# Weighted sums of sampled values by matmuls with matrices of weights, and edge counting in two column halves

## The chip, the cores and the metric

The kernel runs on one core of a Trainium2 chip. TensorE (PE, with its weight loads PEld), VectorE (DVE), ScalarE (ACT), GpSimd (POOL) and SyncE (SP) each work through instructions of their own in order. Transfers are issued by SP, ACT and POOL and run on 16 shared DMA engines. The time is device microseconds of one execution, the median over runs: 6115.38 us over 17 runs before, from 6101.3 to 6127.13.

## The reference

The reference is a network of two blocks on x of 2 images, 64 by 64 places, 256 channels. Each block has a token mixer ("conv") and a feed-forward part ("ffn"), added to x. The change touches the first mixer, a deformable attention, and the first step of the first ffn, a graph attention over 1,048,576 edges.

The first mixer normalizes x, makes queries, keys and values by a matrix and a 3 by 3 depthwise convolution, and has 8 groups of 32 channels. Group g samples keys and values at 9 points around each place, base distance r = 2g + 1, moved by learned offsets, with bilinear weights and clamped coordinates:

```
out = v00 * (1 - wx) * (1 - wy) + v01 * wx * (1 - wy) + v10 * (1 - wx) * wy + v11 * wx * wy
...
k_list.append(_flow_warp(k_map[:, sl], off) * mask[:, None])
v_list.append(_flow_warp(v_map[:, sl], off) * mask[:, None])
...
attn = jnp.einsum('bgpc,bgpkc->bgpk', qh, k)
attn = jax.nn.softmax(attn, axis=-1)
out = jnp.einsum('bgpk,bgpkc->bgpc', attn, v)
...
return out @ proj_w + proj_b
```

The edges' end points are indices of nodes, of which this x has 8192 (2 x 64 x 64). An edge to a higher index is dropped, and a higher source is taken as the last node; the kernel needs, for each node, how many edges with such a source end there.

## The kernel before, in words

`metaformer` (line 2228) runs the parts in order: `attention0`, `project_out`, then the router, the experts and the second block, which the change leaves alone.

**The front** is `static_maps` (209): layernorm and the query, key and value matrix per four tiles of 128 places (228 to 259), then depthwise convolutions, on DVE for queries and values (`dwconv`, 199), on PE for keys (335 to 363), and a convolution on PE that gives offsets and masks (364 to 378). It writes maps to DRAM: `qd`, `kd` (channel, x, image, y), `vd` (rows of both images in turn, with 16 repeated rows and columns as a border) and `offd`. POOL clears the padded query tile q0 (276) and copies the borders of `vd` (`borders`, 309). Between its steps it calls `next(edges)`: `sort_edges` (1047) takes 512 edges a partition at a time, selects words on DVE, and counts nodes: for each edge a one-hot row `ol` of 128 (the node's low 7 bits) and `oh` of 64 (the high bits), in bf16 with 16 edges interleaved, are multiplied into one PSUM tile `psc` (1118). DVE makes `ol` and `oh` (1115, 1116).

**The attention** is `static_attention` (381). If no offset reaches beyond one place, a sample at distance r is a weighted sum over 3 by 3 whole places around it, so each group needs 81 fixed shifts (group 0, whose points adjoin, 25). The groups go in the order 1 to 7, then 0, through three steps, and stage n holds three lanes: values of the nth group, weights of the next, dots of the one after. The lanes' steps are merged by a fraction of the way through each lane (427 to 431), and the framework's scheduler then fixes each engine's order. Two stages come before the first values.

- `group_dots` (440): queries times keys of the same x, for all pairs of rows y and ky: matmuls of 32 rows by 64 columns, 192 moving columns, on four tiles of the array; two images by two halves; ACT copies PSUM into `stage` (480); `store` writes to the DRAM tile `dots`.
- `group_weights` (506): `pick` reads diagonals of `dots` in runs of 32 floats; tents (the bilinear weights) times dots are summed to logits; softmax; POOL multiplies weights and tents into `wt`, 9 by 9 weights a place (`along_x`, 632). Group 0 joins equal shifts (`join`, 638).
- `group_values` (682): for each of 9 row shifts `load` reads the shifted value rows (711); `run` multiplies a window of 16 columns by 3 weights on DVE (733), adds one or two of the three products on POOL (740), and adds the rest into four PSUM accumulators by matmuls with the identity (746). ACT spreads the weights into `wp` (717). `end` copies the sums and stores them in `od`, one row a place (756, 758).

If an offset does reach beyond one place, a loop (`gathered`) computes the attention another way; it doesn't run with these inputs. Its test separates the attention from what follows.

**The projection** is `project_out` (772): per four tiles it loads `od` and x, transposes on PE (790), copies on ACT (792), multiplies (795) and adds to x (796). The layernorm of the router follows it tile by tile.

## Time and profile before

| | |
|---|---|
| median of 17 runs | 6115.38 us (6101.3 to 6127.13) |
| the profiled execution | 6101.96 us, span 6100.2 us |
| busy in the span | PE 4954.1 us (81%), DVE 3728.4 (61%), POOL 2269.2 (37%), ACT 1442.5 (24%) |
| front, 0 to 1005 us | `static_maps` and `sort_edges` |
| two stages without values, 1005 to 1228 us | dots of groups 1 and 2, weights of group 1 |
| eight value stages, 1228 to 3158 us | the groups 1 to 7 and 0 |
| projection, 3158 to 3275 us | with the router's layernorm among it |
| the rest, 3275 to 6100 us | unchanged by the change |

In the lines that follow, a group of instructions is written as line, engine, operation, out<-in, sizes and count, then busy time and mean duration of one in ns, then the idle time of the engine just before them and what ended it. PE's durations contain a part that overlaps the next matmul; the pace is read from starts in order of time. An f32 matmul appears as two PE instructions.

### The profile page before, as it was taken

The page shows a single profiled execution, that of the slowest core. Times are in us where ns is not written, and L with a number is a line of the kernel's source. Part 1 is how long each engine was busy: PE and PEld are TensorE (multiplying, and loading weights), DVE is VectorE, ACT ScalarE, POOL GpSimd, SP SyncE. Part 2 cuts the span into 40 slices and gives each one's busy share as a digit, 9 for nine tenths or more (in the row PEclk, how much of TensorE's full clock was granted, in tenths as well). Part 3 has the DMA queues.
Part 4 walks back from the last instruction along what each step waited for, and adds up shares of the span by engine and source line. Part 5 has one row for each costly group of instructions (what it writes and reads, how often), then busy time and mean ns, then how long its engine had stood idle before and what let it go on. Part 6 is the DMA issues. An engine that isn't in the chain of part 4 may idle for free. (4 is left out here: it accounts for less than half of the span.)

```text
span 6100.2 us, 68586 instructions
## 1 busy us (share of the span) xinstructions
PE 4954.1 (81%) x23911; PEld 2983.2 (49%) x23911; DVE 3728.4 (61%) x6085; ACT 1442.5 (24%) x2580; POOL 2269.2 (37%) x1994
## 2 busy tenths in 40 slices
PE   9999985598998988998877686089976788869993
PEld 5645784333343433433334343078853444448882
DVE  7897866375888887899955577011136555542223
ACT  3221111223333323221003000022223444412220
POOL 0000000064786877788840773700035111110016
PEclk9989986577988978899989798599987888879996
DMA  5436667545546555564243100277742000038885
GB/s 163 147 114 155 135 53 128 122 104 118 131 125 143 126 138 134 143 136 96 59 111 59 7 6 6 104 234 225 225 136 74 21 21 22 21 131 268 262 271 180
DMA packets 946768, 740.49 MB, mean 121 GB/s; under 512 B 611795, under 2 KB 833247, under 8 KB 935265
## 3 DMA queue, kind: packets, MB, share of 16 engines
q1 hardware_dynamic: 725004, 488.35, 32.1%
q10 hardware_dynamic: 185812, 167.81, 10.2%
q0 software_dynamic: 35584, 79.71, 4.4%
q8 instruction: 197, 3.23, 0.2%
q14 instruction: 171, 1.39, 0.1%
HBM read 469.87 MB, written 276.15 MB: 122 GB/s over the span
## 5 line engine op out<-in xcount | busy, mean ns | idle before, releaser
L746 PE MATMUL acc<-prod,ident 128*128 128x512 f32 x2716 | 1389.3, 657 | 156.2 <-POOL prod L740 132.7
L733 DVE TENSOR_TENSOR prod<-vt,wp 128x1536 f32<-128x1536 f32 (+1 forms) x796 | 1334.4, 1732 | 210.3 <-PE acc L746 154.5
L740 POOL TENSOR_TENSOR prod<-prod 128x512 f32<-128x512 f32 x1010 | 1307.0, 1319 | 413.5 <-DVE prod L733 393.4
L746 PEld LDWEIGHTS acc<-prod,ident 128*128 128x128 f32 x2716 | 523.4, 204 | 822.6 <-issue 546.0
L480 ACT COPY stage<-dot 128x384 f32<-128x384 f32 (+1 forms) x640 | 482.8, 840 | 1065.9 <-PE dot L473 868.2
L473 PE MATMUL dot<-kt,qt 32*64 32x192 f32 (+1 forms) x5888 | 511.5, 415 | 154.8 <-ACT stage L480 85.8
L1501 PE MATMUL ps_h<-xgT,w1t 128*128 128x256 f32 x2240 | 540.4, 389 | 33.4 <-DVE xgT L1496 23.8
L473 PEld LDWEIGHTS dot<-kt,qt 32*64 32x64 f32 x5888 | 279.9, 164 | 545.2 <-ACT stage L480 271.1
L1509 PE MATMUL ps_y<-w2t,hT 128*128 128x256 f32 x2240 | 506.3, 379 | 0.0
L1512 DVE TENSOR_TENSOR y<-ps_y,b2t 128x256 f32<-128x256 f32 x280 | 118.8, 424 | 627.3 <-PE ps_y L1509 461.5
L1501 PEld LDWEIGHTS ps_h<-xgT,w1t 128*128 128x128 f32 x2240 | 415.9, 192 | 112.2 <-DVE xgT L1496 33.3
L1509 PEld LDWEIGHTS ps_y<-w2t,hT 128*128 128x128 f32 x2240 | 425.6, 190 | 57.9
L1504 ACT ACTIVATE hT<-ps_h,b1t 128x256 f32<-128x256 f32 x560 | 259.1, 474 | 818.9 <-PE ps_h L1501 752.7
L1234 PE MATMUL ps<-oh,ol 128*128 128x512 f32 (+1 forms) x864 | 328.5, 544 | 93.8 <-DVE oh L1227 93.8
L2127 POOL DMA_INDIRECT xs<-tn,sloti x128 | 124.8, 975 | 611.3 <-DVE slot L2125 522.1
L1596 POOL DMA_INDIRECT back<-ys,back_row x128 | 124.7, 974 | 585.3 <-DVE run L2112 539.7
L207 DVE SCALAR_TENSOR_TENSOR cv<-pad,colt,cv 128x2048 f32<-128x2048 f32 x128 | 296.5, 2339 | 0.0
L1234 PEld LDWEIGHTS ps<-oh,ol 128*128 128x128 f32 x864 | 170.4, 198 | 251.6 <-issue 211.1
L349 PE MATMUL ps_k<-padk,diag 128*128 128x512 f32 x576 | 267.2, 619 | 19.7 <-ACT km L354 19.3
L1494 PE MATMUL ps_x<-ident,xg 128*128 128x128 f32 x560 | 85.7, 276 | 218.3 <-DMA xg<-xs 218.3
L1118 PE MATMUL psc<-oh,ol 128*128 128x64 bf16 x1792 | 239.1, 305 | 22.0 <-DVE oh L1116 22.0
L1118 PEld LDWEIGHTS <-ol 128*128 128x128 bf16 x1792 | 225.2, 148 | 52.2 <-issue 40.9
(392 smaller groups left out, 5961.2 us busy)
## 6 DMA issues: line engine op xcount, KB each, us to landing
w1t<-in_W SPq DMA_DIRECT2D x140, 512.0 KB
w2t<-in_W SPq DMA_DIRECT2D x140, 512.0 KB
xg<-xs SPq DMA_DIRECT2D x140, 256.0 KB
ys<-y ACTq DMA_DIRECT2D x140, 256.0 KB
kt<-kd SPq DMA_DIRECT2D x176, 160.0 KB
pr<-stage SPq DMA_DIRECT2D x16, 1584.0 KB
pad<-pr SPq DMA_DIRECT2D x16, 1122.0 KB
b2t<-in_b SPq DMA_DIRECT2D x140, 128.0 KB
```

The costliest lines, as they stand in the source:

```text
L207: nc.vector.scalar_tensor_tensor(out, src, w, out, ALU.mult, ALU.add)
L349: nc.tensor.matmul(ps.rearrange("p a b -> p (a b)"), lhsT=diag[:, tap, :], rhs=pad[:, at : at + 8, tap % 3 : tap % 3 + W], start=(tap == 0 ...
L473: nc.tensor.matmul(ps[jj][H * b : H * b + H, i, 0 : m * H], lhsT=qt[at, i0 + i, :, b], rhs=kt[at, i0 + i : i0 + i + m, b, :], start=True, ...
L480: (nc.vector.tensor_copy if alone and jj else nc.scalar.copy)(box["d"][:, 0:m, :, x : x + 2].rearrange("p s y i -> p i (s y)"), ps[jj][:, ...
L733: nc.vector.tensor_tensor(pr[:, 0:m], win, wp[:, xh, 0:m, XQ * xq : XQ * xq + XQ].unsqueeze(3).to_broadcast([P, m, XQ, HC]), ALU.mult,)
L740: nc.gpsimd.tensor_tensor(pf[:, 0], pf[:, 0], pf[:, s], ALU.add)
L746: nc.tensor.matmul(box["a"][i].rearrange("p x c -> p (x c)"), lhsT=self.ident, rhs=pf[:, s, :], start=i not in started, stop=last,)
L1118: nc.tensor.matmul(psc, lhsT=ol[:, :, j], rhs=oh[:, :, j], start=(c1 == 0), stop=(c1 == NW - 1),)
L1234: nc.tensor.matmul(psf[:, c : c + m], lhsT=ol, rhs=ohf[:, c : c + m], start=(start and j == 0), stop=(stop and j == n - 1),)
L1501: nc.tensor.matmul(ps, lhsT=w1t[:, k, f * P : (f + 1) * P], rhs=xT[:, k, :], start=(k == 0), stop=(k == CC - 1),)
L1504: nc.scalar.activation(hT[:, f, :], ps, AF.Gelu, bias=b1t[:, f : f + 1])
L1509: nc.tensor.matmul(ps, lhsT=hT[:, f, i * P : (i + 1) * P], rhs=w2t[:, f, :], start=(f == 0), stop=(f == NF - 1),)
```

## The change

The values are summed in another way. The weights of a group are written to a DRAM tile `wd[g]` as matrices: for each x and shift in x, a matrix from source row to output row, whose diagonals hold the weights of the row shifts. All places off the diagonals must be zero, so the matrices are filled with zeros during the front, by 368 transfers from POOL, only in bands around the diagonals. Then a matmul takes the value column of one x (both images, 128 rows by 64: block-diagonal, so that the images stay apart) as weights, and the matrix (128 rows by up to three output columns of 64 rows, elements 384 bytes apart) as the moving operand, and accumulates in PSUM; the two halves of 16 output columns use two column halves of the array. A matrix is loaded by POOL in eight transfers of 16 partitions, into two alternating tiles. Rows that clamp at the upper or lower edge are folded into their neighbours on DVE (`fold`), so `vd` loses its upper and lower border.

The dots now take both images at once: 64 rows (image, channel) by 128 columns (y, image), with queries of the other image set to zero; `dots` lies in another order, so that rows of 96 floats are read back; PSUM has four tiles for it instead of two. Queries, values and the value staging have one tile each. Outputs `od` are stored by channel, so the projection needs no transposes; it now loads all of x and of `od` first. The count of edges exchanges the operands: `oh` (64) are the weights, `ol` (128) moves, and edges go in turn to the lower and upper 64 PSUM partitions, added at the end after a transpose.

The diff, cut to its core:

```diff
@@ static_maps
+            zero = zp.tile([P, 4 * 3 * XH], F32, name="zero")
+            nc.gpsimd.memset(zero, 0.0)
+            def zeros():
+                for g in ORDER:
+                    for y in range(0, H, BAND):
+                        lo, hi = band(g, y)
+                        for b in range(B):
+                            for k in (range(6) if g else (0, 1, 4, 5)):
+                                to = wd[g][y : y + BAND, b, k, lo:hi].rearrange("y (n f) s x -> y n (f s x)", f=4)
+                                ins = nc.gpsimd.dma_start(
+                                    to, zero[0:BAND].unsqueeze(1).to_broadcast([BAND, (hi - lo) // 4, 4 * 3 * XH])
+                                )
...
+                            yield
+            def some(n, after=None):
+                if after is not None:
+                    nc.gpsimd.tensor_copy(tick, after)
+                for _ in range(n):
+                    next(fill, None)
...
                     if i8 % 3 == 0:
                         next(edges)
+                    some(2, st[:, 5, 7, 1:2])
...
-                        to = kd[j * P : (j + 1) * P, :, b, :]
+                        to = kd[j * P : (j + 1) * P, b]
@@ static_attention
-                "prod": pool("atp", 8), "dram": pool("atd", 2, space=DRAM), "wp": pool("atw", 2, space=PSUM),
-                "dot": pool("ats", 2, space=PSUM), "acc": pool("ata", 1, space=PSUM),
+                "dram": pool("atd", 2, space=DRAM), "dot": pool("ats", 4, space=PSUM), "acc": pool("ata", 1, space=PSUM),
...
+            mats = [pools["one"].tile([P, H, 3, XH], F32, name=f"mat{i}") for i in range(2)]
+            pools["vt"] = pools["one"].tile([P, W + 2 * BORDER, B, HC], F32, name="vt")
@@ group_dots
+            qf = qt.rearrange("p x y b -> p (x y) b")
+            nc.vector.tensor_tensor(qf, qf, own.unsqueeze(1).to_broadcast([P, XQ * H, B]), ALU.mult)
...
+                for jj in range(2):
+                    at = slice(64 * jj, 64 * jj + 64)
+                    nc.tensor.matmul(
+                        ps[jj][:, i, :], lhsT=qt[at, i0 + i].rearrange("p y b -> p (y b)"),
+                        rhs=kt[at, i0 + i : i0 + i + 3, :].rearrange("p s y -> p (s y)"), start=True, stop=True,
+                    )
@@ group_weights
+            for sx in range(3):
+                nc.gpsimd.tensor_tensor(
+                    wt[ky][:, sy, :, 2 - sx, :], halves(t5[:, sx, 0, 3 * ky : 3 * ky + 3, :]),
+                    halves(box["wy"][:, sy]), ALU.mult,
+                )
...
+        def fold(i, to):
+            m = FOLDS.index((g, i, to))
+            a = weights(to)
+            nc.vector.scalar_tensor_tensor(a, weights(i), edge[:, m : m + 1], a, ALU.mult, ALU.add)
+        def write(i):
...
+                        dst = bass.AP(
+                            wd.tensor, wd.offset + (lo + d if to is None else to) * stride + b * (stride // B)
+                            + k * block + lo * line,
+                            [[line + (stride if to is None else 0), hi - lo], [block, n], [1, line]],
+                        )
+                        ins = nc.sync.dma_start(
+                            dst, weights(i)[H * b + lo : H * b + hi, k : k + n].rearrange("p k s x -> p k (s x)")
+                        )
@@ group_values
+        def value_map():
+            wb, x0 = W + 2 * (r + 1), BORDER - (r + 1)
+            for x in range(0, wb, 48):
+                n = min(48, wb - x)
+                raw = pools["one"].tile([P, 48, HC], F32, name="raw")
+                nc.sync.dma_start(raw[:, 0:n, :], vd[g].rearrange("b y x c -> (b y) x c")[:, x0 + x : x0 + x + n, :])
+                for b in range(B):
+                    nc.vector.tensor_copy(vt[H * b : H * b + H, x : x + n, b, :], raw[H * b : H * b + H, 0:n, :])
+        def load(n):
+            h, kx, _ = runs[n]
+            for b in range(B):
+                for y in range(0, H, BAND):
+                    lo, hi = band(g, y)
+                    nc.gpsimd.dma_start(mats[n % 2][H * b + y : H * b + y + BAND, lo:hi], wd[y : y + BAND, b, 2 * kx + h, lo:hi])
+        def add(n, j0, j1):
+            h, kx, dx = runs[n]
+            m = mats[n % 2]
+            for j in range(j0, j1):
+                s0, s1 = max(0, 2 - j), min(3, XQ + 2 - j)
+                cuts = [s0] + ([10 - j] if s0 < 10 - j < s1 else []) + [s1]
+                for a, c in zip(cuts, cuts[1:]):
...
+                    for q in range(2):
+                        at = m.offset + a * XH + XQ * q + j - 2 + a
+                        nc.tensor.matmul(
+                            sums[h][64 * q : 64 * q + 64, j - 2 + a : j - 2 + c, :].rearrange("p x y -> p (x y)"),
+                            lhsT=vt[:, r + 1 + XH * h + XQ * q + j + dx].rearrange("p b c -> p (b c)"),
+                            rhs=bass.AP(m.tensor, at, [m.ap[0], [XH + 1, c - a], [3 * XH, H]]),
+                            start=False, stop=last and (j, a) == over,
+                        )
...
-            nc.vector.tensor_tensor(
-                pr[:, 0:m], win,
-                wp[:, xh, 0:m, XQ * xq : XQ * xq + XQ].unsqueeze(3).to_broadcast([P, m, XQ, HC]), ALU.mult,
-            )
...
-                nc.gpsimd.tensor_tensor(pf[:, 0], pf[:, 0], pf[:, s], ALU.add)
...
-                    box["a"][i].rearrange("p x c -> p (x c)"), lhsT=self.ident, rhs=pf[:, s, :],
@@ project_out
+            for t4 in range(0, NT, 4):
+                nc.scalar.dma_start(self.xr[:, t4 : t4 + 4, :], xv[:, t4 : t4 + 4, :])
+            for g in ORDER:
+                at = g % 4 * HC
+                nc.sync.dma_start(oT[g // 4][at : at + HC], od[g * HC : (g + 1) * HC])
...
+                                psy[W * h : W * h + W], lhsT=oT[k][:, b, :, y + h], rhs=wproj[:, k, :],
@@ sort_edges
+                        at = NT * (c1 % 2)
                         nc.tensor.matmul(
-                            psc, lhsT=ol[:, :, j], rhs=oh[:, :, j], start=(c1 == 0), stop=(c1 == NW - 1),
+                            psc[at : at + NT], lhsT=oh[:, :, j], rhs=ol[:, :, j], start=(c1 < 2), stop=(c1 >= NW - 2),
                         )
```

## The prediction

> **What bounds the kernel now.** I read the page first (busy time of each engine, costliest groups), then the busy time by stage, cutting the span where the copies out of the accumulators end, then the groups and waits of one stage, and the order of time where I needed the pace of a single instruction. The groups of 1228 to 3158 us, the value stages, are led by three lines that belong together:
>
> ```profile
> L746 PE MATMUL acc<-prod,ident 128*128 128x512 f32 x2716 | 1389.3, 657 | 156.2 <-POOL prod L740 132.7 <-DVE prod L733 14.4 <-ACT o L756 8.8
> L733 DVE TENSOR_TENSOR prod<-vt,wp 128x1536 f32<-128x1536 f32 (+1 forms) x796 | 1334.4, 1732 | 210.3 <-PE acc L746 154.5 <-ACT wp L717 37.5 <-DMA vt<-vd 17.2
> L740 POOL TENSOR_TENSOR prod<-prod 128x512 f32<-128x512 f32 x1010 | 1307.0, 1319 | 413.5 <-DVE prod L733 393.4 <-PE dot L473 1.0 <-PE acc L746 0.7
> ```
>
> VectorE multiplies, GpSimd adds, TensorE adds the rest through the identity; each waits for the others. By stage (columns: stretch, length, then busy PE, PEld, DVE, ACT, POOL, granted clock, DMA share, GB/s):
>
> ```profile
> 0.00:1005.00 1005.00, 903.68 (x4552) 643.90 (x4554) 799.57 (x1488) 206.43 (x281) 40.49 (x41) 0.91 0.58 126
> 1005.00:1228.00 223.00, 124.78 (x1044) 70.41 (x1040) 104.67 (x164) 55.76 (x71) 4.47 (x5) 0.50 0.53 126
> 1228.00:1601.00 373.00, 326.24 (x1616) 140.79 (x1614) 259.52 (x188) 111.23 (x166) 232.10 (x179) 0.77 0.50 118
> 1853.00:2110.00 257.00, 234.81 (x1129) 98.95 (x1128) 213.85 (x142) 84.33 (x131) 197.22 (x153) 0.89 0.56 134
> ...
> 2854.00:3088.00 234.00, 192.80 (x398) 78.08 (x396) 220.99 (x148) 11.85 (x33) 190.37 (x176) 0.91 0.32 67
> 3088.00:3158.00 70.00, 61.19 (x138) 26.73 (x138) 39.09 (x30) 3.90 (x10) 15.52 (x13) 0.95 0.24 48
> 3158.00:3275.00 117.00, 82.97 (x384) 65.00 (x384) 80.67 (x279) 25.52 (x81) 32.04 (x17) 0.88 0.60 149
> ```
>
> Eight stages take 373, 252, 257, 260, 264, 220, 234 and 70 us, 1930 together. In a full one PE is busy 235 of 257 us, DVE 214, POOL 197: nothing gets shorter unless all three do. The pace of single instructions, in order of time:
>
> ```profile
> 2012.74 0.88 PE L473 MATMUL dot<-kt,qt 32*64 32x192 f32 x16
> 2013.56 7.13 PE L746 MATMUL acc<-prod,ident 128*128 128x512 f32 x16
> ...
> 298.70 2.55 PE L1118 MATMUL psc<-oh,ol 128*128 128x64 bf16 x19
> 301.19 4.04 PE L895 MATMUL ps<-wlo,pc 64*64 64x18 f32 x32
> ...
> 4968.27 1.12 PE L1847 MATMUL ps_o<-v,e 64*64 64x33 f32 x32
> ```
>
> An f32 matmul is two PE passes. A contiguous pass of 512 columns takes 0.435 us, 0.85 ns a column. Sixteen dot passes of 192 columns on four tiles fill 0.65 us, so tiles run side by side, and the next kind of matmul starts 0.81 us after: 0.16 us for the switch. L1118 reads moving columns 32 bytes apart: 0.125 us for 64, 1.95 ns a column. L895 loads 64 weight columns 36 bytes apart and takes 0.12 us; L1847 loads contiguous ones, two tiles at a time, in 0.06 us a pair. So reads with a step cost about 1.9 ns a column, the number that decides here, because the new matmuls read the weights matrix 384 bytes apart.
>
> **A. The value stages (1930 us).** From a full stage (1853 to 2110) go DVE 182 us (108 products), POOL 184 us (144 additions), PE 157 us (361 passes at 0.435), ACT 11 us (27 copies to wp), and 18 value loads of 640 KB.
>
> PE gains, in each of 6 runs, 48 blocks of 64 columns for each column half, two passes: 36,864 columns a stage. At 0.85 ns that is 31 us, at 1.94 ns with the halves side by side 72 us, with the halves in turn 143. I take 72, from the stepped rows. Clearing the sums (8 passes of 0.435) is 3.5 us, 36 switches of 0.16 are 6. The dots become 48 steps of 8 passes on two row halves: 8 x 0.162 / 2 + 0.16 = 0.81 us as before, 39 us. PE: 120 us.
>
> ACT keeps 96 copies of 0.86 (83 us), gains two copies of 1.15 for four of 0.58, keeps 3 us of tents and exp, and issues 24 stores of dots and 8 of outputs at 0.44 to 0.62: 103 us. DVE keeps 214 - 182 = 32, gains 8 folds of 0.76 (row of L602, same size), two query masks of 2.7 and four value copies of about 1.8 (both at L597's 1.3 ns an element): 51. POOL has 27 products for 9, at 0.6 (L649's 128x192 rows lie at 0.6), and 48 loads to issue, between 0.49 (L319) and 1.18 (L314) each: 40 to 72. SP issues some 118 transfers at 0.5: 59. DVE, POOL and SP lie beside PE while they stay under it; uncovered, DVE and POOL would cost what the first stage shows now, half a stage again.
>
> DMA, from the trace's packets: the matrices are 9.3 MB a stage; value loads in packets of 9 to 12 KB moved 14.6 GB/s per engine, 40 us of all 16. Dots 8.5 MB at 16.4 (their stores now): 32. Reading the dots back, 6,912 packets of 384 B at 0.021 us: 9 (20,700 of 128 B before), writing weights much the same: 8. Keys 13, queries 7, values 6, output 4. Together 119 us against 0.56 x 257 = 144.
>
> So three resources stand at 120, 119 and 103. A stage now takes 1.09 of its longest engine (257/235); the two stages with dots only take 1.79 (223/125), with two PSUM tiles for the dots. With loads so even, one query tile, one value tile, and POOL's loads waiting for PE to release a matrix (its products queue behind), I take the middle, 1.4: 168 us. Bounds 131 and 215. Stages: the first 188 (its matrices wait for the last write of weights), four of 168, 150 with the short dots of group 0, 125 without dots, 75 for group 0 alone (54 us of PE and a fill of 20): 1210. The phase is 7.2 such stages. **-720 us** (bounds -985 and -380). PE busy 0.7 of a stage may lose its full clock (0.50 granted at 0.56 busy, 1005 to 1228): the dots would take 78 and PE 159, still inside the bound.
>
> **B. Start-up (1005 to 1228).** PE waits here 85 us for ACT and DVE to empty two PSUM tiles; four tiles take perhaps half of that, the single query tile gives 20 back: **-20** (bounds -60 and +20).
>
> **C. The front (0 to 1005), PE-bound.** The count keeps 1792 matmuls, but 128 stepped columns move instead of 64: 0.25 us each, two column halves side by side, so 0.125 as before: 0. Were the load of 128 weights the limit, the pair would take half, -111; halves in turn, +222, on a PE that is 90% busy. The zero fill is 74.5 MB in 368 POOL transfers of 1.5 KB packets: at 0.050 us, 152 us of all 16 engines on top of 583, all inside 1005. POOL, 40 us busy, needs 180 to 434 us to issue them; the clearing of q0 (now at 296 us) and with it the copies of ACT and the convolutions of DVE queue behind. Key stores change from 256 B to long packets at nearly the same rate, 13.3 and 14.6 GB/s: 0. The fills of the upper and lower border go: 16 short transfers off the path. **+30** (bounds -60 and +250).
>
> The fill leaves 16 partitions at a time. Row: four key loads of 32 partitions ran in flight together at 17.4 GB/s per engine, 278 in all. [...] No row shows a transfer of 16 partitions alone and large; I sum by the row.
>
> **D. Projection (3158 to 3275).** Each block of four tiles started when its own 512 KB was there. Now the first matmul needs all 8.4 MB of outputs, loaded beside 8.4 MB of x: 67 us at 250 GB/s (the stage peaks of before). The transposes and 64 copies go; the DVE work of the stage, 81 us, and of the layernorm among it comes after: 162 for 117. **+45** (bounds +10 and +80).
>
> **Sum.** -720 - 20 + 30 + 45 = -665 on the profiled execution's 6101.96 (span 6100.2): 5437. That execution lies 13 us under the median of the 17 runs, 6115.38, so the forecast for the median is **5450**.
>
> **Rivals.** (1) Stages run as tight as now: 1.09 x 120 = 131, 985 us saved, 5185. For it: four PSUM tiles, fewer small packets; against: no engine leads, so all wait. (2) The column halves read in turn: PE 192, times 1.15, 221 a stage, 1591 for the phase, 5830. For it: the halves of L473 overlap with contiguous reads only, and no row shows two stepped moving streams. (3) The fill holds up the front: +240 instead of +30, 5660; for it the DMA share of 0.7 between 700 and 1000 us, against it that POOL and half the DMA time are free. (4) Slower: one step of 384 bytes costs more than one of 32. With the other terms at +55, a stage breaks even at 260 us, PE at 238, so at 5.1 ns a column; at 7.8 (four times the row) PE needs 336, a stage 366, the phase 2635, and the time is 6875. Against: 32 and 36 bytes cost the same. (5) The matrices come too slowly to matter, all else gained is lost to waits: about 6100.
>
> **How the numbers follow.** Forecast 0.51, (1) 0.15, (2) 0.13, (3) 0.09, (4) 0.10, (5) 0.02. The forecast alone spans 5250 to 5650. The range reaches to (1) and over (2) and the bound of C: 5080 to 5950, leaving out (4) and the tails. About 0.2% is what a measurement tells from no change: faster 0.88, same 0.01, slower 0.11.
>
> **What would show it.** Right: the three lines above gone; value matmuls of 192 columns starting in pairs about 0.37 us apart; stages of 150 to 190 us led by no engine; DMA share 0.65 to 0.8. Wrong: pairs 0.16 apart (too slow a forecast), 0.75 apart (2), more (4); ACT's and DVE's waits in the front ending on the clearing of q0 (3); POOL's loads landing late, with PE waiting for matrices, would lengthen A beyond its bound.

## The result, and the profile after

The changed kernel takes 6323.81 us (median of 8 runs, 6301.8 to 6334.31) where the kernel before took 6118.2 on the same occasions: a ratio of 1.0336, interval 1.0323 to 1.0349. It is slower by 3.4%; the forecast was 5450 us. Its profiled execution has a span of 6313.1 us against 6100.2, 213 us more. Cut at the first sustained dot products, the first value matmul, the last copy of a value sum and the end of the projection, the difference is made up like this (the prediction cut the kernel before at 1005 where the dots begin at 990, which moves 15 us between the first two rows and nothing else):

| stretch | before | after | difference | predicted |
|---|---|---|---|---|
| front, to the first dots | 990 | 1684 | +694 | C: +30 |
| start-up, to the first value matmul | 238 | 238 | 0 | B: -20 |
| eight value stages | 1930 | 1432 | -498 | A: -720 |
| projection | 117 | 136 | +19 | D: +45 |
| all behind it | 2825 | 2823 | -2 | 0 |

So most of what the value stages were to give came, and the front took it back with interest. First the four groups that stand where the products and additions stood (same columns as the costliest groups of before):

```profile
L534 PE MATMUL dot<-kt,qt 64*128 64x192 f32 x2944 | 476.7, 419 | 647.4 <-DVE qt L518 269.9
...
L847 PE MATMUL acc<-mat,vt 128*64 128x192 f32 (+2 forms) x3680 | 499.8, 439 | 117.5 <-DMA mat<-wd 117.5
...
L825 POOL DMA_DIRECT2D mat<-wd x368 | 178.9, 492 | 910.6 <-PE acc L847 535.1
...
L259 POOL DMA_DIRECT2D wd<-zero x368 | 197.5, 540 | 350.4 <-DMA wd<-zero 332.6
```

The multiplications on DVE, the additions on POOL and the identity matmuls are gone. What replaced them on PE, the matmuls with matrices (L847), is 500 us for eight stages, 62 a stage. POOL now loads matrices, and waits mostly for PE to release one, and it issues the zero fill, during which it waits 332.6 us for earlier transfers of the fill. By stage (busy PE, PEld, DVE, ACT, POOL, granted clock, DMA share, GB/s):

```profile
0.00:1684.00 1684.00, 956.37 (x4467) 599.03 (x4467) 828.75 (x1549) 200.79 (x277) 260.15 (x425) 0.74 0.75 117
1684.00:1922.00 238.00, 114.45 (x738) 95.72 (x739) 115.98 (x146) 72.47 (x92) 26.50 (x44) 0.68 0.48 128
1922.00:2038.00 116.00, 103.31 (x716) 70.68 (x714) 41.73 (x51) 41.86 (x60) 29.00 (x50) 0.90 0.73 154
2038.00:2301.00 263.00, 158.04 (x1016) 113.03 (x1016) 49.17 (x59) 93.76 (x137) 44.25 (x85) 0.77 0.66 148
...
2491.00:2709.00 218.00, 138.44 (x918) 94.72 (x915) 47.08 (x55) 77.63 (x114) 40.77 (x75) 0.78 0.78 170
...
3354.00:3490.00 136.00, 57.44 (x512) 55.74 (x512) 32.96 (x98) 3.11 (x5) 31.59 (x17) 0.71 0.53 131
```

The first row is the loss. PE is busy 956 us there, DVE 829, ACT 201, against 893, 791 and 202 in the 990 us before: about the same work. The DMA engines are busy 75% of 1684 us, 1263 us, where they were busy 57% of 990, 564 us, and they move 117 GB/s on average, less than the 124 of before, while they are so busy. The waits of the front say who stands still (engine, line, what for: us in total, times, longest):

```profile
POOL tick L272 <- ACT stage L306: 545.0, 15, 68.5
DVE cv L227 <- DMA pad<-pr: 360.3, 6, 139.6
...
POOL wd L259 <- DMA wd<-zero: 332.6, 176, 6.7
...
ACT vt L351 <- DMA vd<-vt: 239.1, 10, 115.3
...
ACT stage L306 <- DMA pr<-stage: 183.0, 6, 45.8
...
DVE rounds L1272 <- POOL topa L1271: 175.1, 1, 175.1
...
PE dot L534 <- DVE qt L518: 115.5, 1, 115.5
...
DVE qt L518 <- DMA edge<-in_fold: 87.0, 1, 87.0
```

The first and third lines are POOL's own pacing: it issues the fill in small lots behind other engines' steps. The second, fourth and fifth are engines that wait for a transfer: DVE for the padded rows of the convolutions, ACT for stores of the projection and of the transposed values, so that it can write their tiles again. All are on other queues than the fill.

The last three lines belong to the end of the front and are of another kind, POOL being late. The reduction of the edge sort (L1271) runs at 1594 us, as it stands behind most of the fill and the value map's borders in POOL's order. The last 30 or so transfers of the fill are issued behind it, from 1594 to 1664 us, and PE, idle from 1569 to 1684, waits for them too: its first dots need the masked queries, these need the mask's factors (`edge`), and SP could load `edge` only when the last zeros had landed:

```profile
SPq L449 <- DMA wd<-zero: 72.7, 3, 69.3
```

The transfers between 1200 and 1500 us, the DMA engines' share in 40 slices and by queue:

```profile
DMA  9999999999986606999999999966999999999994
...
q0 software_dynamic: 5168, 17.61, 57.4%
q1 hardware_dynamic: 112181, 10.26, 40.6%
```

The engines are busy in nearly every slice, at 96 GB/s. Queue q0, which carries the fill, holds 57% of the engines' time to move 17.6 MB. In the trace of the packets most of the fill's are 4608 bytes long and last 0.74 us each in the median, 6.2 GB/s per engine; a packet of another queue takes as long as it did before (2112 bytes: 0.089 us, 0.088 before). So what the others lose is time before their packets' turn, which the records of the packets don't hold; the runs below test it. Over the front the fill's packets sum to 716 us of all 16 engines. The prediction had 152.

### The profile page after: what moved, and what is told of

Same layout as the page of the kernel before. It is cut to its first block, busy times and chain, and to the rows that moved or that the text cites. A ratio compares the mean times of both kernels' runs of the same rounds, so it can differ in the third digit from the quotient of the medians.

```text
span 6313.1 us, 63607 instructions
## 1 busy us (share of the span) xinstructions
PE 4139.7 (66%) x22124; PEld 2835.7 (45%) x22124; DVE 2491.0 (39%) x5448; ACT 1325.4 (21%) x2302; POOL 1393.8 (22%) x1856
## 5 line engine op out<-in xcount | busy, mean ns | idle before, releaser
L534 PE MATMUL dot<-kt,qt 64*128 64x192 f32 x2944 | 476.7, 419 | 647.4 <-DVE qt L518 269.9
L534 PEld LDWEIGHTS dot<-kt,qt 64*128 64x128 f32 x2944 | 379.9, 234 | 754.2 <-issue 519.9
L541 ACT COPY stage<-dot 128x384 f32<-128x384 f32 x640 | 444.4, 853 | 865.8 <-PE dot L534 443.5
L847 PE MATMUL acc<-mat,vt 128*64 128x192 f32 (+2 forms) x3680 | 499.8, 439 | 117.5 <-DMA mat<-wd 117.5
L847 PEld LDWEIGHTS acc<-mat,vt 128*64 128x64 f32 x3680 | 311.1, 159 | 301.8 <-issue 219.6
L825 POOL DMA_DIRECT2D mat<-wd x368 | 178.9, 492 | 910.6 <-PE acc L847 535.1
L1231 PE MATMUL psc<-ol,oh 128*64 128x128 bf16 x1792 | 236.1, 422 | 115.5 <-DVE oh L1228 114.5
L302 PE MATMUL ps_q<-xT,wq 128*128 128x512 f32 x384 | 217.8, 707 | 90.9 <-ACT stage L306 80.0
L259 POOL DMA_DIRECT2D wd<-zero x368 | 197.5, 540 | 350.4 <-DMA wd<-zero 332.6
L1231 PEld LDWEIGHTS <-oh 128*64 128x64 bf16 x1792 | 178.0, 201 | 189.1 <-DVE oh L1228 143.7
```

What stands on the lines that cost most here:

```text
L259: ins = nc.gpsimd.dma_start(to, zero[0:BAND].unsqueeze(1).to_broadcast([BAND, (hi - lo) // 4, 4 * 3 * XH]))
L302: nc.tensor.matmul(ps.rearrange("p a b -> p (a b)"), lhsT=wq[:, k, c * P : (c + 1) * P], rhs=xT[:, k, :], start=(k == 0), stop=(k == CC - 1),)
L534: nc.tensor.matmul(ps[jj][:, i, :], lhsT=qt[at, i0 + i].rearrange("p y b -> p (y b)"), rhs=kt[at, i0 + i : i0 + i + 3, :].rearrange("p s y ...
L541: (nc.vector.tensor_copy if alone and jj else nc.scalar.copy)(box["d"][:, :, :, x : x + 2].rearrange("p y s i -> p i s y"), ps[jj].rearran ...
L847: nc.tensor.matmul(sums[h][64 * q : 64 * q + 64, j - 2 + a : j - 2 + c, :].rearrange("p x y -> p (x y)"), lhsT=vt[:, r + 1 + XH * h + XQ * ...
L1231: nc.tensor.matmul(psc[at : at + NT], lhsT=oh[:, :, j], rhs=ol[:, :, j], start=(c1 < 2), stop=(c1 >= NW - 2),)
```

## The experiments

The runs were made on five chips. The kernel before takes 6397 to 6403 us on four of them and 6113 on the fifth, where only the writes by POOL's queue were run; the result's 6118 is near the fifth. On the slower four the edge stage and the experts are longer (in before_count on one of them the edge stage's matmuls are busy 363.9 us for 328.5, with 245.5 us of idle time before them for 93.8, and the experts' first ones 552.4 for 540.4); up to the end of the value stages the two kinds agree within 1% (3158 and 3182 us, the second with the edit of the count in it). So times below are ratios to the kernel before on the same chip, and stretches up to the last value sum are compared in us.

The theories: (1) the fill's source, 16 partitions, makes its packets slow, and the engine time of these starves the front; (2) the 74.5 MB written are the cost, whatever their source; (3) POOL's order delays others; (4) the count or the new layouts slow the front; (5) the number of transfers does.

**The source of the fill, every eighth partition.** One slice is changed: the zeros come from 16 partitions as before, but spread over all 128.

```
-    to, zero[0:BAND].unsqueeze(1).to_broadcast([BAND, (hi - lo) // 4, 4 * 3 * XH])
+    to, zero[0:P:8].unsqueeze(1).to_broadcast([BAND, (hi - lo) // 4, 4 * 3 * XH])
```

> The kernel after, with the fill's source on every eighth partition (0, 8, ..., 120) in place of 0 to 15; number of transfers, partitions, packets and bytes all stay. [...] Theory 1 in a loose form (the number of partitions, 16, sets it): packets 0.74 us and time within 40 us of 6324. Rival 2 (bytes) and rival 5 (number of transfers): time within 40 us of 6324.

The front's row of it:

```profile
0.00:1426.00 1426.00, 954.50 (x4467) 599.35 (x4467) 830.43 (x1549) 200.60 (x277) 255.83 (x423) 0.79 0.62 139
```

Measured: packets of 0.374 us for 0.74, 334 us of the 16 engines instead of 716, the front 258 us shorter, at 1426; 6344 us against 6403 for before, from a single run. Same number of transfers, partitions, packets and bytes, and the same order on POOL: theory 1 holds, though not in its loose form, as it matters which 16 partitions they are; rivals 2, 3 and 5 fall for this part of the loss. The front's end still waits for the last fills, with PE idle for 75.8 us before its first dots.

**The fill from 96 partitions.** The rows of y, image and tap merge to 192, so that a transfer can take 96 of them. 64 transfers instead of 368, 78.4 MB instead of 74.5 since group 0's two unused blocks are filled too.

```
-    for b in range(B):
-        for k in (range(6) if g else (0, 1, 4, 5)):
-            to = wd[g][y : y + BAND, b, k, lo:hi].rearrange("y (n f) s x -> y n (f s x)", f=4)
+    rows = wd[g][y : y + BAND].rearrange("y b k o s x -> (y b k) o s x")
+    for at in (0, 96):
+        to = rows[at : at + 96, lo:hi].rearrange("r (n f) s x -> r n (f s x)", f=4)
...
-    to, zero[0:BAND].unsqueeze(1).to_broadcast([BAND, (hi - lo) // 4, 4 * 3 * XH])
+    to, zero[0:96].unsqueeze(1).to_broadcast([96, (hi - lo) // 4, 4 * 3 * XH])
```

> The kernel after, with the zero fill issued as 64 transfers of 96 partitions (32 rows at a time were 16 partitions in 368 transfers); the bytes and the packets' size stay, only the source's partitions change. Theory 1 (the source's 16 partitions make each 4.6 KB packet last 0.74 us, and the 740 us of all 16 engines that this makes starve the front): packets fall to 0.17 to 0.30 us, the fill's share to 170 to 300 us, the front (to the first dot products) from 1684 to 1000 to 1200 us, the time from 6324 to 5640 to 5850. Rival 2 (the 74.5 MB written to HBM are the cost, whatever their source): packets stay near 0.74 us and the time above 6200. Rival 3 (the order on POOL: the ticks and the clearing of q0 queued behind the fill): packets get shorter, but the front stays above 1450 and the time above 6080.

```profile
0.00:1213.00 1213.00, 935.63 (x4475) 595.96 (x4475) 833.33 (x1555) 204.06 (x279) 108.84 (x120) 0.86 0.69 167
1213.00:1450.00 237.00, 111.46 (x728) 96.18 (x728) 111.52 (x140) 71.02 (x90) 30.98 (x45) 0.67 0.48 126
1450.00:2884.00 1434.00, 892.03 (x5948) 604.99 (x5950) 311.90 (x382) 407.02 (x588) 302.46 (x565) 0.78 0.75 150
```

Measured: packets of 0.178 us in the median, 271 us of the 16 engines, ratio 0.9572 (0.9549 to 0.9596). The median packet times 0.74, 0.374 and 0.178 us halve from one source to the next; in the mean, 0.71, 0.33 and 0.255, the last step is smaller. By what way the partitions set the time, these runs don't show. The front, at 1213, is 223 us longer than before's, though: a little beyond what was expected, and more than nothing. Not all of that is the fill, whose last packet starts at 583 us. PE idles 65.6 us before its first dots (15 before the change), because in SP's order the load of the queries comes behind the end of the edge sort:

```profile
1213.03 3.22 PE L534 MATMUL dot<-kt,qt 64*128 64x192 f32 x17 [65.57 <-DVE qt L518]
```

```profile
1201.10 0.33 SPq L1266 DMA_DIRECT2D left<-hand  x1
1203.28 1.72 SPq L515 DMA_DIRECT2D qt<-qd  x4
```

The value stages are what they were, 1434 us: the fill didn't hold those up.

**The fill alone, in the kernel before.** The same 368 transfers at the same places, into a tensor that nothing reads.

> The kernel before, with the fill alone added: same 368 transfers, at the same places in the program, into a DRAM tensor that nothing reads. Theory 1 and rival 2: front 990 to 1500 to 1700 us, time 6118 to 6600 to 6850. Rival 4 (the count, the transposed query, key and value maps or the other small edits of the front make most of the 694 us): time under 6400.

```profile
0.00:1606.00 1606.00, 958.88 (x4462) 652.86 (x4462) 826.97 (x1547) 198.71 (x273) 221.15 (x388) 0.73 0.74 116
1606.00:2091.00 485.00, 269.72 (x2196) 153.76 (x2196) 107.58 (x133) 140.76 (x187) 39.36 (x55) 0.50 0.61 140
2091.00:3871.00 1780.00, 1607.22 (x6411) 670.71 (x6412) 1561.79 (x1035) 432.23 (x710) 1424.49 (x1122) 0.90 0.50 114
```

Measured: 7112 us against 6403, from a single run. The fill alone makes the front 616 us longer (theory 1 had 510 to 710). It also lengthened the start-up from 238 to 485 and let the value stages be 150 shorter: the start-up holds 2196 PE instructions where before's had 1140, and the value stages 6411 for 7484, so more of the dots were done ahead of the first values. What made the first values late was not taken apart. Of the 694 us of the change, 78 are left. The wait at the end of its front covers them: here the dots begin at 1606 with 73 us of the fill's engine time still to come, while in the change they wait for the last of it, and PE idles 115 us. Nothing points to the change's other edits in the front.

**The count alone, in the kernel before.** The two column halves of L1231, and the turn at the end that adds them.

```
+    at = NT * (c1 % 2)
-    psc, lhsT=ol[:, :, j], rhs=oh[:, :, j], start=(c1 == 0), stop=(c1 == NW - 1)
+    psc[at : at + NT], lhsT=oh[:, :, j], rhs=ol[:, :, j], start=(c1 < 2), stop=(c1 >= NW - 2)
```

> The kernel before, with the edge count's two column halves alone changed. The trace after has a pair of halves every 0.232 us (0.116 a matmul, 0.125 before) over work that lies beside the projection, so theory 1 expects a ratio of 0.997 to 1.003 and a front of 980 to 1000 us. Rival 4 expects more than 1.005 and a front over 1020 us.

```profile
0.00:982.00 982.00, 910.39 (x4466) 583.85 (x4466) 786.47 (x1471) 202.74 (x277) 35.92 (x33) 0.95 0.56 123
...
1250.00:3182.00 1932.00, 1742.81 (x7461) 733.28 (x7456) 1579.70 (x1061) 511.93 (x817) 1415.69 (x1122) 0.86 0.51 118
```

Measured: 1.0017 (1.0004 to 1.0031), front 982. The halves do run side by side: in the trace after, the two of a pair start about 7 ns apart, a pair every 0.232 us. Theory 4 falls for the count.

**Two tiles of queries.** With the front explained, the missing 222 us of the value stages (1432 for 1210). One of PE's waits in them is for dots whose queries are late. The first group shown above has 269.9 us of it, but that counts the front's last wait and the start-up; from 1922 to 3354 us it is 108, beside 136 for keys, 125 for ACT's copies of dots and 118 for matrices. Here the queries get a second buffer and are asked for one run earlier; to make room, the value map comes in 16 columns at a time, the output tile in halves and one tile of products along y goes.

```
-    box["q"] = qt = pools["one"].tile([P, XQ, H, B], F32, name="qt")
+    box[h] = qt = two.tile([P, XQ, H, B], F32, name="qt")
```

> The 96-partition fill, with the queries' tile double-buffered and the second half's queries asked for one run earlier (room for it: the value map's raw tile 16 wide in place of 48, the output tile in two halves, one wy tile). In the value stage of after at 2491 to 2709 us PE lay idle about 80 of 218 us, 27 to 57 of it while the queries waited for their tile, their DMA and their mask. Theory A1 (the single tile of queries holds the stage): a stage of the middle falls from 213 to 175 to 195 us and the eight stages from 1434 to 1150 to 1300; ratio to before 0.957 to 0.915 to 0.940. Rival A2 (the DMA engines, busy 78%, most of all by the matrices' loads from 16 partitions, hold it) and rival A3 (PE's own 138 us and the order of the steps): eight stages above 1390, ratio above 0.950.

```profile
1134.00:1397.00 263.00, 132.39 (x729) 106.98 (x729) 144.98 (x224) 72.88 (x92) 40.33 (x47) 0.62 0.49 124
1397.00:2856.00 1459.00, 905.12 (x5952) 603.51 (x5952) 319.00 (x432) 410.01 (x604) 301.63 (x565) 0.77 0.75 147
```

Measured: 0.9563 (0.9536 to 0.959) against 0.9572: nothing. The value stages are 25 us longer. PE's wait for queries fell from 110 to 37 us in them, and its wait for ACT's copies of dots rose from 124 to 230: the wait moved, and theory A1 falls. The front is 79 us shorter, and the start-up 26 longer: in this version the first queries are loaded ahead of the sort's end, and with the whole fill in it the front is 144 us longer than before's instead of 223.

**Matrix loads into every fourth partition.** The matrices' rows go to the partitions in the order (y in a band, image, band), so that one load of both images takes every fourth partition; the value map follows, and its two copies become products with a column of zeros and ones.

```
-    nc.gpsimd.dma_start(mats[n % 2][H * b + y : H * b + y + BAND, lo:hi], wd[y : y + BAND, b, 2 * kx + h, lo:hi])
+    rows = wd[y : y + BAND, :, 2 * kx + h].rearrange("y b o s x -> (y b) o s x")
+    nc.gpsimd.dma_start(mats[n % 2][y // BAND : P : H // BAND, lo:hi], rows[:, lo:hi])
```

> The 96-partition fill, with the matrices laid out in SBUF so that each load reaches every fourth partition, 32 of them, both images at once (bytes the same, half as many transfers; the value map follows the same order of partitions). The loads' packets of 12 to 18 KB last 1.25 to 2.2 us at 8.4 to 10 GB/s per engine from 16 neighbouring partitions. By theory 1 they fall to 0.5 to 1.0 us, and the loads' 58 us of the 16 engines per middle stage to 20 to 30. Rival A2 then gains: eight stages 1434 to 1200 to 1340, ratio 0.92 to 0.945. Theory A1 and rival A3: packets fall, stages stay within 40 of 1434, ratio 0.950 to 0.960.

```profile
0.00:1181.00 1181.00, 937.05 (x4475) 595.78 (x4475) 833.50 (x1555) 204.25 (x279) 109.91 (x120) 0.87 0.70 171
...
1415.00:2675.00 1260.00, 884.24 (x5960) 614.45 (x5960) 319.74 (x385) 404.64 (x588) 230.94 (x389) 0.82 0.60 171
```

Measured: 0.9271 (0.9253 to 0.929). A packet of 18,432 bytes went from 2.32 to 0.686 us, one of 12,288 from 1.34 to 0.466, 26 to 27 GB/s per engine; the DMA share of the value stages went from 0.75 to 0.60, and the stages from 1434 to 1260. PE's wait for matrices fell from 112 to 60 us, and that for keys, which come on SP's queue, from 107 to 24. Rival A2 was right: 16 neighbouring partitions, slow as a source, are slow as a destination too. The 174 us are the price of the loads as they were; as there are half as many now, POOL's time for issuing them also fell, from 178 to 98 us, and the run doesn't separate the two.

**The products along x on DVE.** In that kernel a middle stage still has two stretches with PE nearly idle. In order of time, POOL, SP's queue and PE around the second of them:

```profile
2108.11 12.88 POOL L707 TENSOR_TENSOR wt<-tents,wy 128x192 f32<-128x192 f32 x18 [39.36 <-DVE wy L700]
2139.00 5.02 POOL L707 TENSOR_TENSOR wt<-tents,wy 128x192 f32<-128x192 f32 x9 [18.01 <-DMA kt<-kd]
2176.86 4.23 POOL L827 DMA_DIRECT2D mat<-wd  x8 [32.84 <-DMA tents<-offd]
```

```profile
2126.09 9.05 SPq L747 DMA_DIRECT2D wd<-wt  x5
...
2148.93 23.70 SPq L747 DMA_DIRECT2D wd<-wt  x13
...
2181.91 10.86 SPq L599 DMA_DIRECT2D tents<-offd  x7
```

```profile
2131.94 13.29 PE L536 MATMUL dot<-kt,qt 64*128 64x192 f32 x80 [19.09 <-DVE qt L520]
2156.14 10.71 PE L536 MATMUL dot<-kt,qt 64*128 64x192 f32 x64 [10.91 <-ACT stage L543]
2190.50 2.17 PE L849 MATMUL acc<-mat,vt 128*64 128x64 f32 x14 [23.65 <-DMA mat<-wd]
```

The products that spread the next group's weights (L707, 0.70 us each) start at 2108, and what ended POOL's idle time before them is DVE's wy, the end of the softmax (L700), not the loads of this group; their writes follow on SP until 2173; the next matrices are loaded at 2177, and PE, out of dots since 2167, has its first value matmul at 2190. The experiment issues the 27 products of a group on DVE.

```
-    nc.gpsimd.tensor_tensor(
+    nc.vector.tensor_tensor(
         wt[ky][:, sy, :, 2 - sx, :], halves(t5[:, sx, 0, 3 * ky : 3 * ky + 3, :]),
         halves(box["wy"][:, sy]), ALU.mult,
     )
```

> The kernel with 96-partition fill and wide matrix loads; the 27 products a group that spread the weights along x (0.68 us each on POOL) go to DVE, so that they no longer stand behind the matrices' loads in POOL's order. In that kernel's trace the middle stages repeat one chain: products on POOL 188 to 224 us from 1920, the writes of the weights 206 to 253, the next matrices' loads 256 to 264, the first value matmul 278; PE is nearly idle from 193 to 278. Theory A4 (a group's weights are made, written, and read back one after another, and PE waits for that) in the form that POOL's order starts the chain late: value stages 1260 to 1050 to 1180, ratio 0.927 to 0.895 to 0.915. If POOL's order isn't what starts it (the logits' reads on SP's queue are), stages within 40 of 1260, ratio 0.92 to 0.932.

The group in the kernel with wide loads, then here, and the value stages here:

```profile
L707 POOL TENSOR_TENSOR wt<-tents,wy 128x192 f32<-128x192 f32 x216 | 142.8, 697 | 499.4 <-DVE wy L700 260.2 <-ACT stage L543 142.4 <-DMA kt<-kd 64.7
```

```profile
L707 DVE TENSOR_TENSOR wt<-tents,wy 128x192 f32<-128x192 f32 x216 | 62.1, 356 | 53.0 <-DMA wd<-wt 35.1 <-DMA kt<-kd 17.4 <-issue 0.4
```

```profile
0.00:1191.00 1191.00, 939.52 (x4475) 596.88 (x4475) 833.43 (x1555) 204.04 (x279) 109.81 (x120) 0.87 0.70 170
...
1421.00:2639.00 1218.00, 885.74 (x5960) 611.71 (x5960) 351.20 (x573) 405.22 (x588) 108.19 (x200) 0.83 0.62 176
```

Measured: 0.9205 (0.9187 to 0.9223), the fastest version of all. The stages fell by 42 us, to 1218, at the edge of the second expectation: POOL's order isn't what starts the chain, as the line of POOL above had shown. A product costs 0.356 us on DVE for 0.697, which fits the gain: in the stage shown the way from wy (2107.2) to the first value matmul (2190.5) took 83.3 us, and here the same way takes 78.0 (2100.0 to 2178.0), 5.3 us less; eight times that is 42.

**The weights' writes on another queue.** If SP's queue carried the rest, taking the writes off it (22 a group in the trace, not the 37 of the expectation) should free the reads of the next group. Once by ACT (products on POOL as before), once by POOL, where the second diff line reads nc.gpsimd (products on DVE).

```
-    ins = nc.sync.dma_start(
+    ins = nc.scalar.dma_start(
         dst, weights(i)[H * b + lo : H * b + hi, k : k + n].rearrange("p k s x -> p k (s x)")
     )
```

> The same kernel, with the weights' writes issued by ACT's queue in place of SP's. In a middle stage SP issues some 37 writes at a mean of 0.93 us over 47 us, and the next group's offsets, logits and keys are read only behind them. Theory A4 in the form that SP's queue carries the chain: value stages 1260 to 1050 to 1200, ratio 0.927 to 0.895 to 0.918. If not: within 40 of 1260, or slower where ACT's copies of the dot products now stand behind the writes (up to +40 a stage, ratio up to 0.97).

> 96-partition fill, wide matrix loads, the weights' products along x on DVE, and the weights' writes issued by POOL's queue, which now holds only matrix loads, in place of SP's. In the run with the products on DVE, SP still issues a group's writes over 205 to 261 us of a middle stage and reads the next group's offsets only behind them (261 to 279), and PE waits meanwhile. If SP's queue carries the chain: value stages 1218 to 1020 to 1150, ratio 0.9205 to 0.890 to 0.910. If not (the writes wait for the folded weights wherever they are issued, and POOL's own cost of issuing 384-byte rows adds to the chain): 1190 to 1320, ratio 0.915 to 0.94.

Measured: by ACT 0.9297 (0.9281 to 0.9312), value stages 1294 for 1260; by POOL 0.9241 (0.9219 to 0.9262), 1259 for 1218. Neither is faster than with SP. By ACT the interval overlaps that of the kernel it is compared with (0.9253 to 0.929); by POOL it is slower (462 us less than before on its chip, where the products on DVE had given 515). So taking the writes off SP does not shorten the stage; since they then stand before other work of ACT or POOL, a gain and a loss may hide each other. What paces the stage stays open.

**The fill in other places.** Left of the front's loss are some 200 us with a fill of 271 us of engine time. Three runs move it. In the first, with both edits above (two tiles of queries, wide loads), the fill of five of the eight groups is moved into the value stages.

> Both edits at once, and only the first three of the eight groups' fill (29 of 79 MB) left in the front; the fill of each later group is issued three stages ahead, in the value stages. Theory 1 for the front: to the first dot products 1195 falls to 1030 to 1110 us (990 before the change), at a price of about 20 us of DMA time in each of five stages. Value stages: 1150 to 1300 if A1 and A2 both count. Ratio to before 0.87 to 0.92. If neither counts and the fill only moves, 0.94 to 0.96.

Measured: 0.9366 (0.9348 to 0.9385). The front fell to 1047, but all five groups were filled as the dots began, since nothing held them back, and the start-up grew to 400 us at a DMA share of 0.74. In the second the fill of a group waits for the value map of the stage, and the two tiles of queries are left out:

```
+    def hold():
+        nc.gpsimd.tensor_scalar(zero[:, 0:1], pools["vt"][:, 0, 0, 0:1], 0.0, None, ALU.mult)
```

> The kernel with 96-partition fill and wide matrix loads, only three of eight groups' fill in the front, and each later group's fill held back by a data dependence on the value map of the stage three ahead of its use (without that, in the run before, all five groups' fill was issued at once as the dots began, and the start-up grew from 252 to 401 us). Front to the first dot products 1040 to 1080 (1163 with the whole fill there), start-up 240 to 270, value stages 1260 to 1300; ratio 0.905 to 0.918. If the fill's 79 MB cost the same wherever they go: 0.925 to 0.935.

```profile
0.00:1089.00 1089.00, 913.07 (x4469) 586.56 (x4471) 833.47 (x1555) 204.10 (x279) 76.55 (x81) 0.90 0.59 135
1089.00:1369.00 280.00, 118.53 (x728) 97.95 (x727) 108.98 (x138) 70.34 (x90) 41.55 (x54) 0.65 0.63 177
1369.00:2707.00 1338.00, 888.31 (x5957) 615.10 (x5957) 313.92 (x393) 404.07 (x588) 252.13 (x416) 0.80 0.65 187
```

Measured: 0.9277 (0.9261 to 0.9292), the same as with all of the fill in the front (0.9271). The front is 92 us shorter, the start-up 46 and the value stages 78 longer: 124 us for the 181 us of engine time that were moved there. In the third, with the products on DVE, none of the fill is issued before the key convolution, and two transfers behind each of its tiles:

> The kernel with 96-partition fill, wide matrix loads and the products along x on DVE, and the same 79 MB of fill held back until the key convolution (two transfers behind each of its 32 output tiles, by a data dependence), nothing in the projection loop. In the runs with the fill in 96 partitions the projection loop ends at 414 to 440 us (295 without the fill) with the DMA engines busy 75 to 78%, while from 600 to 900 us PE works 298 of 300 us at 140 GB/s. Theory (what was left of the front's loss, 170 to 205 us, is fill taken from the projection loop's transfers, and the same bytes hide beside the key convolution): first dot products 1173 to 1000 to 1080, start-up and value stages unchanged (248 and 1218), ratio 0.9205 to 0.895 to 0.912. Rival (the bytes cost the same wherever they go, as they did in the value stages): first dot products 1140 to 1200, ratio 0.915 to 0.93.

By stretches of the front, first with the fill in the projection loop (the kernel with wide loads), then with the late fill:

```profile
0.00:300.00 300.00, 215.50 (x845) 115.69 (x846) 167.28 (x531) 64.90 (x116) 40.84 (x58) 0.84 0.78 239
...
600.00:900.00 300.00, 297.91 (x1502) 193.37 (x1500) 253.99 (x362) 49.66 (x62) 15.46 (x13) 1.00 0.61 140
```

```profile
0.00:300.00 300.00, 278.48 (x1153) 152.22 (x1155) 238.09 (x775) 93.02 (x162) 7.86 (x11) 0.95 0.44 148
300.00:600.00 300.00, 221.61 (x815) 120.67 (x812) 212.00 (x127) 55.81 (x39) 67.77 (x52) 0.82 0.73 233
600.00:900.00 300.00, 237.85 (x1207) 155.21 (x1206) 194.85 (x326) 29.80 (x40) 40.27 (x47) 0.90 0.83 203
```

Measured: 0.926 (0.924 to 0.9281) against 0.9205. The projection loop ends at 299 us instead of 420, but the key convolution takes 518 us instead of 352: PE, at 298 of 300 us in the first fence's second row, is at 238 in the second one's third. The fill costs about half to two thirds of its engine time in all three places (121 us less in the projection loop and 166 more in the key convolution, for 257 to 271 of engine time), though the share of the DMA engines leaves room in each.

## Why the prediction was wrong, point by point

**C, the front, failed, by its largest term.** The term was the zero fill, "at 0.050 us, 152 us of all 16 engines", and it measured 716. No run shows that price: 1.5 KB in 0.050 us are 30.7 GB/s per engine, and the fastest large packets in the trace of before moved 26.8 (32,768 bytes in 1.22 us). It isn't the row's either: "I sum by the row" names 32 partitions at 17.4 GB/s per engine, by which the term would be 268 us. The packets came out at 4608 bytes and 6.2 GB/s, because of the 16 neighbouring partitions they start from, which no row of before had shown for large packets; fill_ports8 and fill_96 show that the partitions of the source decide (0.374 and 0.178 us for 0.74). By itself the right price would not have been enough: 716 us and the 564 of the front before, passed without a gap, are 1280, an estimate from the two traces, and the front took 1684.

The second failure in C is "all inside 1005": even the fill from 96 partitions, at 271 us of engine time, made the front 223 us longer (144 where the queries come ahead of the sort's end), and fill_late shows it again in the stretch that looked freest. A share of 0.58 was read as room for 0.42 more. It wasn't: the front is a sequence of loads, convolutions and stores, and a transfer that comes later because the engines hold other packets is late for the engine behind it: in fill_96 DVE waited 144.1 us for the tiles of x, before the change 9.5. With the slow source nearly the whole engine time came on top: 616 us for 638 in before_fill.

The third, a smaller one, is in the order of the queues, which C looked at for the clearing of q0 alone. The dots wait for what stands behind the fill: PE idles 115 us at the end of the front, for the sort's reduction on POOL and then for the last zeros.

The rival (3), "the fill holds up the front", was the right mechanism with the wrong place: it named the clearing of q0, and it named POOL. q0 was indeed cleared at 793 us instead of 322 (the prediction's 296 is POOL's idle time before it), but because the ticks before it waited for ACT's copies in the projection loop, and these for transfers. Its +240 was a third of the loss. Rival (4) has the sign of the result, but not its cause: a step of 384 bytes costs no more than one of 32 (below). Nor did (1), (2) or (5) happen.

The count's 0 was right: 0.116 us for 0.125 a matmul, and 1.0017 alone.

**A, the value stages, was right in direction and short by 222 us.** -498 for -720, inside the bounds. By its terms: a value matmul of 192 columns takes 0.325 us a pair where 0.37 was expected, so a step of 384 bytes costs 1.69 ns a column, less than the 32-byte row's 1.95, and PE has 62 us of them for 72. The halves start 5 to 7 ns apart, so rival (2) had no ground. The dots were 60 us a stage for 39: 0.162 us a pass for 0.10, although the two row tiles do start together, 7 ns apart. The next two follow 0.16 or 0.27 us later while the granted clock is 1.0, and 0.32 us later while it is 0.5, so a part is the clock, for which the prediction had 78 us in reserve; the value matmuls keep 0.325 us a pair at either clock. What turns 0.16 into 0.27 was not tried. PE was busy 138 of 218 us for the 120 estimated. DMA was 170 us for 119 (0.78 of 218 us), and that is where the size was lost: matrices were priced by value loads at 14.6 GB/s per engine, and into 16 partitions they moved 9.9 in the mean, 57 us a stage for 40; the stores of dots took 45 for 32. Loads into every fourth partition gave back 174 of the 222 us, and the products along x, which the prediction put beside PE, another 42, as they were not beside it: they lie in the chain from the softmax to the matrices' loads, for which PE waits. With both, the stages are 1218 for 1210, which is in part luck, as the sum agrees better than its parts do: the first stage of after takes 116 us for 188, the second 263 for 168.

**B** was 0 for -20, and **D** +19 for +45: both inside their bounds.

**The shape of the forecast.** A, B and D ended inside their bounds; with them as measured and C at its +30 the median would have been 5664 (6115 - 498 + 19 - 2 + 30), inside the range. C's upper bound was +250; +694 means that nearly all of the fill's 716 us came on top.

## What to carry to other kernels

Count the partitions, and which ones, at both ends of every large transfer before pricing it by a row: nearly the same bytes took 716, 334 and 271 us of the DMA engines from 16 neighbouring, 16 spread and 96 partitions. Bulk transfers aren't free because their queue is idle and the engines' share is 0.6; where a stage waits for its own transfers one after another, they cost a good part of their engine time wherever they are put (here half to two thirds, and nearly all with the slow source), so the way to save is fewer bytes or other partitions, not another place. What stands behind a bulk transfer in a queue's order comes late with it (PE idled 115 us at the end of the front); look for what the next stage needs first. A wait that is removed may come back as another: the second tile of queries gave nothing, while the loads' partitions and products on POOL that looked covered gave 216 us.

## What the runs showed of the hardware

- Which SBUF partitions a transfer touched set its rate, reading and writing alike: packets of 4608 bytes took 0.74, 0.374 and 0.178 us in the median (6.2, 12.3 and 25.9 GB/s per engine) from partitions 0 to 15, from every eighth and from 96 in a row, and packets of 18,432 bytes 2.32 us into 16 neighbouring partitions and 0.686 us into every fourth.
- Slow packets on one queue held up the others without changing their packets' own time (2112 bytes: 0.088 and 0.089 us): the fill alone made the front 616 us longer, and from 1200 to 1500 us the 16 engines were busy at 96 GB/s.
- Two column halves with stepped moving reads of 384 bytes ran side by side at 1.69 ns a column (192 columns in 0.325 us), at a granted clock of 0.5 as at 1.0, and bf16 ones of 32 bytes at 0.116 us for 128 columns in pairs.
- The same product of 128x192 f32 took 0.697 us on POOL and 0.356 on DVE.

The version that comes out of this (fill from 96 partitions, matrix loads into every fourth partition, products along x on DVE) takes 0.9205 of the time before, and with it the sums by matmuls are worth having: 1218 us of value stages for 1930, for a front that is 201 us longer.
